# Four head pairs of attention between changes of the matmul tiling, in place of two, in a hand-ordered transformer block

## The chip, the cores and the metric

The kernel runs on one core of a Trainium2 chip. The metric is device time in microseconds for one launch; smaller is better. The core has five engines, each with its own queue, which it works off in the order written: TensorE (PE in the profile, with its weight loads as PEld), VectorE (DVE), ScalarE (ACT), GpSimd (POOL), and SyncE (SP), which only issues DMAs. An instruction waits for semaphores of other engines, and everything behind it in its queue waits with it.

## The reference

Input x has 8 batches of 512 rows of 256 floats. Four residual blocks follow each other, each behind a layer norm:

```python
x = x + attn_a(ln(x))   # Q,K,V = x W; Q,K l2-normalised; Q * mean over rows of (K*V)
x = x + ffn(ln(x))      # r = sigmoid(xr W_r); k = relu(xk W_k)^2; r * (k W_v)
x = x + attn_b(ln(x))   # 16 heads of 64; softmax over the *queries* (axis=2)
x = x + ffn(ln(x))      # the same weights as the first ffn
```

In the ffn, xr and xk mix each row with the row before it. In `attn_b`, scores are q.k/8, the softmax runs over the query axis for each key, and the 16 head outputs are joined and projected from 1024 to 256 columns. All is float32. `attn_b` has 8 x 16 heads of 512 x 512 scores and is the largest part.

## The kernel before

**Attention.** Heads are worked in pairs, 8 pairs to a batch, 64 pairs in all. A pair is four steps of 128 keys. In one step `scores` (L1262) issues 64x64-tiled matmuls that put two heads' scores, keys by queries, into one PSUM tile of two banks; VectorE finds the maximum of each row for both heads with one reduction of 1024 (L1279); `exps` (L1284) has ScalarE write two exponentials of 512 and their sums (L1290). Since the softmax runs over the queries, the sums belong to keys: `scale_v` (L1298) divides the values by them, a reciprocal on VectorE (L1303) and a product on GpSimd (L1307). `context` (L1314) multiplies scaled values and exponentials in two more banks, and after the fourth step ScalarE copies one (L1334) and VectorE adds the other (L1335). Three score tiles of two banks and the two context banks fill PSUM; full-size matmuls borrow free tiles, one bank of each.

**Everything else** is full-size (128x128) matmuls: `linear` and `queries` (the first attention, L678, L728), `mean` (L748), `ffn` (L559), its second use called the tail (`tail`, L1218), with first products for both halves in `keys` (L600), `project_pairs` (L949: queries and keys of two pairs), `values_fast` (L989) and `project_out_fast` (L1118). The last four use a seven-product scheme of Strassen's kind (`seven`, L893): seven products of half size replace eight, differences of inputs are made beforehand on GpSimd, and the results are put together by ScalarE and VectorE while a bank is used twice. A batch's row differences (`sums_of_rows`, L856, L872) lie in `xts`, of which there is one buffer; those of the context (`differences`, L1090, L1102, and `last_differences`, L1105, L1111) overwrite buffers that the tail uses. Rows are turned into columns through DMA transposes that SP issues (L450, L1205), with copies on GpSimd before and after (L445, L454, L1200, L1209).

**The order.** TensorE must change its tiling between attention and the rest. The main loop (L1397) takes two pairs at a time: `attend` (L1340) issues eight steps of scores, and the contexts four or five steps behind; then full-size work is issued, then the next two pairs. Which full-size work comes, and how all engines' instructions interleave, is decided when the program is built, by the class `Order` (L104): each piece of work is a chain of steps with an engine, an assumed cost and the time at which it may start; `PLAN` gives each kind of chain a due stretch and a lead; `CHOICES` gives each stretch a budget shift and picks that depart from the rule. Nothing is decided on the chip.

```python
for first in range(0, G, 2):
    attend(first)
    ...
    order.add(project_pairs(g + 1), "pairs", g)
    ...
    order.until(g, share)
```

`p` is a pair's number in its batch. Before, two pairs are projected in every stretch; the out-projection of batch b-1 and the second half of the values of b come behind p = 1, the first half of the next batch's values behind p = 3, with due times two and four stretches later.

## Time and profile before

| | us |
|---|---|
| median of 3 runs (lowest, highest) | 1130.21 (1129.76, 1130.29) |
| the profiled execution's own time | 1131.28 |
| its span | 1129.5 |
| TensorE busy | 1108.6 |
| VectorE busy | 784.5 |
| ScalarE busy | 675.3 |
| GpSimd busy | 588.6 |
| DVE reductions L1279, 256 of 1216 ns | 307.7 |
| GpSimd scaled values L1307, 128 of 613 ns | 78.3 |

The page gives busy times by engine, the span in 40 slices, the chain of work that ended last, and groups of instructions by line with what ended the idle time before them. Each float32 matmul stands as two records. The 64x64 records overlap four at a time, and the ends of matmuls are modelled, so lengths are best read from start to start.

### The profile page before, as it was taken

How to read it: one execution, taken by the hardware profiler on the slowest of the kernel's cores; microseconds unless marked ns; L12 is line 12 of the kernel's file. 1: busy time of each engine (PE TensorE's matmuls, PEld its weight loads, DVE VectorE, ACT ScalarE, POOL GpSimd, SP SyncE). 2: the span in 40 equal slices, each digit the busy share in tenths (PEclk: the TensorE clock that was granted, in tenths of full speed). 3: DMA queues.
4: the chain of work that ended last, by engine and by line, in shares of the span. 5: the costliest groups of instructions: out<-in, count | busy, mean ns of one | idle time of the engine just before them, and what ended most of it. 6: DMA issues, size and time to landing. Idle time of an engine off the chain costs nothing. (4 is left out here: it accounts for less than half of the span.)

```text
span 1129.5 us, 19476 instructions
## 1 busy us (share of the span) xinstructions
PE 1108.6 (98%) x6938; PEld 691.4 (61%) x6938; DVE 784.5 (69%) x1487; ACT 675.3 (60%) x1779; POOL 588.6 (52%) x909
## 2 busy tenths in 40 slices
PE   7999999999999999999999999999999999999997
PEld 4655556664756657666567656575565765655556
DVE  5767777668576785777856777657776677765764
ACT  4657656377455773567645776547774377554653
POOL 3594445554465464665557546476553764344311
PEclk9999999999999999999999999999999999999999
DMA  6020100110101111112011110111110111001101
GB/s 228 13 82 11 28 1 10 29 29 11 29 30 38 20 20 29 39 29 29 10 38 38 24 23 17 51 20 38 20 19 20 27 31 20 1 20 28 20 1 38
DMA packets 83424, 34.16 MB, mean 30 GB/s; under 512 B 73088, under 2 KB 81920, under 8 KB 82816
## 3 DMA queue, kind: packets, MB, share of 16 engines
q1 hardware_dynamic: 82432, 31.87, 12.5%
q8 instruction: 55, 0.90, 0.3%
q10 hardware_dynamic: 864, 1.05, 0.3%
q14 instruction: 41, 0.34, 0.1%
q0 software_dynamic: 32, 0.00, 0.0%
HBM read 10.89 MB, written 4.19 MB: 13 GB/s over the span
## 5 line engine op out<-in xcount | busy, mean ns | idle before, releaser
L1290 ACT ACTIVATE e<-sc,nm 128x512 f32<-128x512 f32 x512 | 346.5, 690 | 140.1 <-DVE nm L1279 139.9
L1279 DVE TENSOR_REDUCE nm<-sc 128x2 f32<-128x1024 f32 x256 | 307.7, 1216 | 48.5 <-PE sc L1274 47.6
L1274 PE MATMUL sc<-qk 64*64 64x512 f32 x2048 | 265.1, 593 | 4.6 <-DVE prev_g L486 1.3
L1327 PE MATMUL cx<-e,vs 64*64 64x512 f32 x2048 | 263.6, 590 | 0.8 <-POOL vs L1307 0.5
L1307 POOL TENSOR_TENSOR vs<-v,rs 128x256 f32<-128x256 f32 x128 | 78.3, 613 | 266.2 <-DVE rs L1303 256.5
L1327 PEld LDWEIGHTS cx<-e,vs 64*64 64x64 f32 x2048 | 85.0, 133 | 136.5 <-issue 113.4
L1274 PEld LDWEIGHTS sc<-qk 64*64 64x64 f32 x2048 | 75.3, 132 | 139.6 <-issue 79.6
L1290 ACT ACTIVATION_READ_ACCUMULATOR e<-sc,nm 128x1 f32 x512 | 105.9, 207 | 0.0
L972 ACT ACTIVATE qk<-m_qk,bias 128x256 f32<-128x256 f32 x124 | 51.9, 473 | 45.2 <-PE m_qk L964 45.1
L1335 DVE TENSOR_TENSOR ctx<-cx,ctx 128x512 f32<-128x512 f32 x64 | 44.2, 691 | 47.9 <-ACT ctx L1334 39.5
L980 DVE SCALAR_TENSOR_TENSOR qk<-m_qk,dbias,qk 128x256 f32<-128x256 f32 x124 | 54.1, 478 | 16.7 <-PE m_qk L964 14.3
L699 PE MATMUL kv<-wkv,xrFalse 128*128 128x512 f32 x112 | 53.8, 612 | 0.0
L445 POOL COPY xrFalse<-xnFalse 128x512 uint16<-128x512 uint16 x72 | 41.7, 611 | 8.8 <-ACT xnFalse L418 8.8
L1334 ACT COPY ctx<-cx 128x512 f32<-128x512 f32 x64 | 37.5, 586 | 11.1 <-PE cx L1327 11.1
L454 POOL COPY xrFalse<-xkFalse 128x1024 uint16<-128x1024 uint16 x24 | 31.7, 1337 | 22.8 <-DMA xkFalse<-xrFalse 22.8
L1145 PE MATMUL m_y<-ctx,al 128*128 128x256 f32 x168 | 39.8, 380 | 0.0
L964 PE MATMUL m_qk<-xta,aq 128*128 128x256 f32 x124 | 39.3, 398 | 0.1
L964 PE MATMUL m_qk<-xta,sums_q 128*128 128x256 f32 x124 | 37.7, 386 | 0.3 <-DVE qk L926 0.3
L964 PE MATMUL m_qk<-xts,aq 128*128 128x256 f32 x124 | 37.4, 383 | 0.3 <-DVE qk L916 0.3
L964 PE MATMUL m_qk<-xts,ak 128*128 128x256 f32 x124 | 36.9, 379 | 0.0
L964 PE MATMUL m_qk<-xta,ak 128*128 128x256 f32 x124 | 36.9, 379 | 0.0
L964 PE MATMUL m_qk<-xta,sums_k 128*128 128x256 f32 x124 | 36.9, 379 | 0.0
(272 smaller groups left out, 2119.6 us busy)
## 6 DMA issues: line engine op xcount, KB each, us to landing
out<-x SPq DMA_DIRECT2D x16, 256.0 KB, 2.1
x<-in_x SPq DMA_DIRECT2D x6, 512.0 KB, 4.1
aq<-in_aq SPq DMA_DIRECT2D x1, 1024.0 KB, 7.2
ak<-in_ak SPq DMA_DIRECT2D x1, 1024.0 KB, 9.3
av<-in_av SPq DMA_DIRECT2D x1, 1024.0 KB, 11.4
al<-in_al SPq DMA_DIRECT2D x1, 1024.0 KB, 5.3
xkFalse<-xrFalse SPq DMA_TRANSPOSE x36, 3.1
x<-in_x ACTq DMA_DIRECT2D x4, 128.0 KB, 4.2
```

The source lines that it names most:

```text
L445: nc.gpsimd.tensor_copy(apart.rearrange("p (l k u d) -> p l k u d", l=2, k=KC, u=2)[:, :, :, u, :], xn[:, u, :].rearrange("p (k d l) -> p ...
L699: nc.tensor.matmul(ps, lhsT=xt[:, kc, u * P : (u + 1) * P], rhs=wkv[:, kc, :], start=(kc == 0), stop=(kc == KC - 1),)
L964: nc.tensor.matmul(ps[:, w * HS : (w + 1) * HS], lhsT=lhs[w][n - 1], rhs=block_of_rows(b, n), start=start and w == 0, stop=True, skip_grou ...
L972: nc.scalar.activation(dst[:, w, :], ps[:, w, :], AF.Identity, bias=bias[:, w, p : p + 1])
L980: nc.vector.scalar_tensor_tensor(dst[:, w, :], ps[:, w, :], dbias[:, w, p // 2 : p // 2 + 1], part[:, w, :], ALU.add, ALU.add,)
L1145: nc.tensor.matmul(ps, lhsT=lhs[n - 1][:, g, :], rhs=rhs[g][n - 1], start=first and g == 0, stop=True, skip_group_check=True,)
L1274: nc.tensor.matmul(ps[m * HD : (m + 1) * HD, j, :], lhsT=kt[hs, keys], rhs=qt[hs, :], start=True, stop=True,)
L1279: nc.vector.tensor_reduce(nm, ps, AX.X, ALU.max, negate=True)
L1290: nc.scalar.activation(e[:, j, :], ps[:, j, :], AF.Exp, bias=nm[:, j : j + 1], accum_out=sums[g, h][:, c % 2, j : j + 1],)
L1307: nc.gpsimd.tensor_tensor(vs, vh[b, p // 4][:, 2 * h : 2 * h + 2, cols].rearrange("p t (j d) -> p t j d", j=2), rs.unsqueeze(3).to_broadca ...
L1327: nc.tensor.matmul(cx[m][j * HD : (j + 1) * HD, :], lhsT=vsc[g, c // 2][ks, c % 2, j, :], rhs=es[g, c][ks, j, :], start=(c == 0), stop=(c ...
L1335: nc.vector.tensor_tensor(ct, cx[1], ct, ALU.add)
```

## The change

- The main loop takes four pairs between two stretches of full-size work, except the first two and the last two pairs. `attend(first, n)` holds any number of pairs; a pair's contexts run one step behind the next pair's scores.
- Both `project_pairs` of four pairs come in one stretch, so there are four query/key buffers (`heads`). With stretches behind pairs 1 and 5 alone, the first half of the next batch's values comes behind p = 5, and both halves are due at once.
- PSUM is eight tiles of one bank. A score step takes two of them, and its maximum is two reductions of 512 in place of one of 1024.
- To make room, squares are written over a tile that a later product fills, in place of a scratch tile; one set of `sums` is left out; the value bias is loaded in quarters into `vb` and `dvb`, which a subtraction later turns into a difference; the output bias is loaded late, into the room of `sums_y`, and added by a chain of its own (`biased`).
- `CHOICES` is a new table of 18 rows, one to a stretch. With it the order of nearly all instructions is new.

```diff
@@ -28,6 +28,7 @@
 FFN = 1.1 + 6 * BANK
 FAST = BANK / 2
 CHANGE = 0.1
+STEPS = 18
 PAIRS, BANKS = 3, 2
 X_LANDS = (4.1, 8.5, 12.0)
 PASS = {"T": 0.27, "A": 0.2, "V": 0.17, "G": 0.17, "S": 2.2}
...
@@ -64,9 +62,9 @@
     "ffn 0": (-1, 8), "ffn 1": (-3, 8), "ffn": (-3, 8),
     "norm 0": (-1, 8), "norm 1": (-3, 8), "norm": (-3, 8),
     "rows": (-1, 8), "tail": (15, 0), "keys": (15, 0), "tail last": (17, 16), "tail 6": (17, 0), "keys 6": (17, 0), "pairs": (0, 8),
-    "values 1": (2, 8), "values 0": (4, 8), "y": (0, 8), "y differences": (0, 8),
-    "y rows": (4, 8), "y plain": (2, 0), "y last": (11, 16), "scale": (0, 128),
-    "v 0": (-1, 0), "v 1": (3, 0), "project": (-1, 0), "sums": (0, 0), "late sums": (5, 0), "sums v": (1, 0),
+    "values 1": (0, 8), "values 0": (0, 8), "y": (0, 8), "y differences": (0, 8),
+    "y rows": (4, 8), "y plain": (2, 0), "y last": (11, 16), "scale": (0, 128), "bias": (5, 0),
+    "v 0": (-1, 0), "v 1": (1, 0), "project": (-1, 0), "sums": (0, 0), "late sums": (5, 0), "sums v": (1, 0),
 }
 
 class Steps:
...
@@ -154,9 +152,13 @@
 
     def take_pair(self):
 
-        self.clear(range(PAIRS))
-        since, i = min((t, i) for i, t in enumerate(self.banks[:PAIRS]))
+        self.clear(range(2 * PAIRS))
+        since, i = min((max(self.banks[2 * i : 2 * i + 2]), i) for i in range(PAIRS))
         return i, since
+
+    def keep_pair(self, i, until):
+
+        self.banks[2 * i : 2 * i + 2] = [until, until]
 
     def give(self, i=None):
 
...
@@ -293,7 +295,7 @@
     small = ctx.enter_context(tc.tile_pool(name="small", bufs=7))
     epool = ctx.enter_context(tc.tile_pool(name="epool", bufs=5))
     cpool = ctx.enter_context(tc.tile_pool(name="cpool", bufs=9))
-    heads = ctx.enter_context(tc.tile_pool(name="heads", bufs=2))
+    heads = ctx.enter_context(tc.tile_pool(name="heads", bufs=4))
     psum = ctx.enter_context(tc.tile_pool(name="psum", bufs=1, space=bass.MemoryType.PSUM))
     halves_v = ctx.enter_context(tc.tile_pool(name="halves_v", bufs=4))
     ctx.enter_context(tc.manual_schedule())
...
@@ -338,28 +340,26 @@
     aq = weight("aq", [P, KC, H * HD], nc.sync)
     ak = weight("ak", [P, KC, H * HD], nc.sync)
     av = weight("av", [P, KC, H * HD], nc.sync)
-    vb = const.tile([P, H * HD], F32, tag="vb", name="vb")
-    lb = const.tile([P, 1, D], F32, tag="lb", name="lb")
+    vb = const.tile([P, 2, 2 * P], F32, tag="vb", name="vb")
 
     lc = const.tile([P, KC], F32, tag="lc", name="lc")
     dlc = const.tile([P, 1], F32, tag="dlc", name="dlc")
     dbias = const.tile([P, 2, NP // 2], F32, tag="dbias", name="dbias")
     dvb = const.tile([P, 2, 2 * P], F32, tag="dvb", name="dvb")
-    nc.sync.dma_start(out=vb, in_=a["vb"].partition_broadcast(P))
+    for half in range(2):
+        for dst, at in ((vb, 0), (dvb, 1)):
+            cols = slice((2 * half + at) * 2 * P, (2 * half + at + 1) * 2 * P)
+            nc.sync.dma_start(out=dst[:, half, :], in_=a["vb"][cols].partition_broadcast(P))
     nc.sync.dma_start(out=bias[:, 0, :], in_=a["qb"])
     nc.sync.dma_start(out=bias[:, 1, :], in_=a["kb"])
-    nc.sync.dma_start(out=lb[:, 0, :], in_=a["lb"].partition_broadcast(P))
     nc.sync.dma_start(out=lc, in_=a["lb"].rearrange("(k p) -> p k", p=P))
 
 
     def psum_tile(i, name):
...
@@ -703,8 +704,9 @@
             ready = yield "A", 0.8, ready
             vs = two.tile([P, D], F32, tag="av", name=f"av_{b}_{h}_{u}")
             nc.scalar.copy(vs, ps[:, D:])
-            sq = one.tile([P, D], F32, tag="sq", name=f"sqk_{b}_{h}_{u}")
-            nc.scalar.activation(sq, ps[:, :D], AF.Square, accum_out=ss[:, u : u + 1])
+            nc.scalar.activation(
+                kv[:, u, :], ps[:, :D], AF.Square, accum_out=ss[:, u : u + 1]
+            )
             if u == 1:
                 order.add(queries(b, h), *due_of("queries", b))
...
@@ -811,9 +813,13 @@
                 add_front(b + 1)
 
         if b == B - 1:
-            yield "G", 1.3, ready
-            xh = xb[:, 2 * h : 2 * h + 2, :]
-            nc.gpsimd.tensor_tensor(xh, xh, lb.to_broadcast([P, 2, D]), ALU.add)
+            order.add(biased(b, h, ready), "bias", NP * b)
+
+    def biased(b, h, ready):
+
+        yield "G", 1.3, ready, -1, "lb"
+        xh, lb = x[b][:, 2 * h : 2 * h + 2, :], blocks["sums_y"][:, 0:1, :D]
+        nc.gpsimd.tensor_tensor(xh, xh, lb.to_broadcast([P, 2, D]), ALU.add)
 
 
...
@@ -1188,6 +1199,10 @@
                 out=al.rearrange("p (g i) d -> p g i d", i=2)[:, :, 0, P:],
                 in_=a["al"].rearrange("p (g i) d -> p g i d", i=2)[:, :, 0, P:],
             )
+            nc.sync.dma_start(
+                out=blocks["sums_y"][:, 0, :D], in_=a["lb"].partition_broadcast(P)
+            )
+            order.marks["lb"] = p4 + 2.5
         order.add(rows_of_output(b, 0, max(c11, c21)), "y rows", NP * b + 9)
 
     def rows_of_output(b, h, ready):
...
@@ -1266,20 +1281,21 @@
         if c % 2 == 0:
             sums[g, h] = small.tile([P, 2, 2], F32, tag="sums", name=f"sums_{g}_{h}")
         i, since = order.take_pair()
-        ps = psum_tile(i, f"sc_{g}_{c}")
+        ps = [psum_tile(2 * i + j, f"sc_{g}_{c}_{j}") for j in range(2)]
         for m in range(2):
             keys = slice(c * P + m * HD, c * P + (m + 1) * HD)
             for j in range(2):
                 hs = slice(j * HD, (j + 1) * HD)
                 nc.tensor.matmul(
-                    ps[m * HD : (m + 1) * HD, j, :], lhsT=kt[hs, keys], rhs=qt[hs, :],
+                    ps[j][m * HD : (m + 1) * HD, :], lhsT=kt[hs, keys], rhs=qt[hs, :],
                     start=True, stop=True,
                 )
         nm = small.tile([P, 2], F32, tag="nm", name=f"nm_{g}_{c}")
-        nc.vector.tensor_reduce(nm, ps, AX.X, ALU.max, negate=True)
+        for j in range(2):
+            nc.vector.tensor_reduce(nm[:, j : j + 1], ps[j], AX.X, ALU.max, negate=True)
         ready = order.place("T", 0.86, max(since, order.marks[f"qk_{g - g % 2}"]))
-        scored[g, c] = i, ps, nm, order.place("V", 1.14, ready)
-        order.banks[i] = 1e9
+        scored[g, c] = i, ps, nm, order.place("V", 1.2, ready)
+        order.keep_pair(i, 1e9)
 
     def exps(g, c):
 
...
@@ -1335,30 +1351,26 @@
             nc.vector.tensor_tensor(ct, cx[1], ct, ALU.add)
             ctxt[divmod(g, NP)] = ct
             ready = order.place("A", 0.5, ready)
-            order.banks[PAIRS:] = [ready, order.place("V", 0.62, ready)]
-
-    def attend(g):
-
-        for c in range(NT):
-            if c == 3:
-                order.at_once(scale_v(g, 0))
-            scores(g, c)
-            if g > 0:
-                context(g - 1, c)
-            else:
-                order.fill(BANK)
-            exps(g, c)
-            order.fill(0.0, 1.0)
-        for c in range(NT):
-            scores(g + 1, c)
-            if c == 1:
-                order.at_once(scale_v(g, 1))
-            if c > 0:
-                context(g, c - 1)
-            if c == 3:
-                context(g, 3)
-            exps(g + 1, c)
-            order.fill(0.0, 1.0)
+            order.banks[2 * PAIRS :] = [ready, order.place("V", 0.62, ready)]
+
+    def attend(first, n):
+
+        for g in range(first, first + n):
+            behind = 1 if g > first else 0
+            for c in range(NT):
+                if c == 3 and g < first + n - 1:
+                    order.at_once(scale_v(g, 0))
+                scores(g, c)
+                if c == 1 and g > first:
+                    order.at_once(scale_v(g - 1, 1))
+                if g > 0 and c >= behind:
+                    context(g - 1, c - behind)
+                elif g == 0:
+                    order.fill(BANK)
+                if behind and c == 3:
+                    context(g - 1, 3)
+                exps(g, c)
+                order.fill(0.0, 1.0)
 
 
     G = B * NP
...
@@ -1394,10 +1404,13 @@
     total -= 17 * 1.1 + 7 * 1.1
     total += 2 * FAST - 7 * FAST / 2
     total -= 7 * 2 * FAST
-    for first in range(0, G, 2):
-        g = order.period = first + 1
+    first = 0
+    while first < G:
+        n = 2 if first in (0, G - 2) else 4
+        g = order.period = first + n - 1
+        order.step += 1
         order.place("T", CHANGE, 0.0)
-        attend(first)
+        attend(first, n)
         order.place("T", CHANGE, 0.0)
         order.open = g
         for h in range(2):
@@ -1407,19 +1420,21 @@
             order.add(project_out(b, 0), "y plain", g)
         if p == 1 and b > 0:
             order.add(project_out_fast(b - 1), "y", g)
-        if g + 1 < G:
-            order.add(project_pairs(g + 1), "pairs", g)
+        for i in (1, 3):
+            if g + i < G:
+                order.add(project_pairs(g + i), "pairs", g)
         if p == 1 and b > 0:
             order.add(values_fast(b, 1), "values 1", g)
-        elif p == 3 and b < B - 1:
+        elif p == 5 and b < B - 1:
             order.add(values_fast(b + 1, 0), "values 0", g)
-        share = (total - order.spent) / ((G - first) // 2) + order.choice[0]
+        share = (total - order.spent) * n / (G - first) + order.choice[0]
         begin = order.spent
         order.until(g, share)
         if g < G - 1:
             order.fill(share - (order.spent - begin), 1.0 + order.choice[1])
 
             order.fill(order.marks[f"qk_{g + 1}"] - order.now)
+        first += n
 
     order.fill(order.free["G"] - order.now, 4.0)
```

## The prediction

> **What bounds the kernel now.** I read the page's busy times and slices first, then the chain that ended last, then stretches of the span cut at each change of tiling, then the timelines of VectorE and GpSimd.
>
> ```profile
> span 1129.5 us, 19476 instructions
> ...
> PE 1108.6 (98%) x6938; PEld 691.4 (61%) x6938; DVE 784.5 (69%) x1487; ACT 675.3 (60%) x1779; POOL 588.6 (52%) x909
> ...
> PE   7999999999999999999999999999999999999997
> ```
>
> TensorE is busy from end to end. Nothing can be won but its own gaps and what it pays to change its tiling. The chain of work shows that payment:
>
> ```profile
> 901.38 1.02 PE sc L1274 x8
> ...
> 1001.77 1.72 PE cx L1327 x16
> 1003.48 1.06 PE m_v L1001 x4
> 1004.54 1.73 PE m_y L1145 x8
> 1006.27 0.86 PE m_v L1001 x4
> ```
>
> A piece of four 256-wide matmul records takes 0.86 and eight 64x64 records also take 0.86 (1.72 for sixteen); the first piece after a change takes 1.02 or 1.06. So entering the small tiles costs 0.16 and leaving them 0.20. Stretches tell where more is lost:
>
> ```profile
> 258.45:267.86 9.41, 8.54 (x40) 6.52 (x37) 7.76 (x22) 7.56 (x18) 5.87 (x12) 1.00 0.14 27
> 406.28:420.17 13.89, 13.89 (x129) 4.77 (x128) 10.77 (x13) 11.86 (x32) 8.85 (x16) 1.00 0.11 21
> 556.21:587.45 31.24, 31.24 (x132) 24.24 (x128) 18.80 (x43) 14.82 (x42) 15.10 (x26) 1.00 0.09 18
> 601.35:625.72 24.37, 24.37 (x117) 21.19 (x113) 14.71 (x37) 9.39 (x22) 20.98 (x34) 1.00 0.13 26
> 670.92:679.30 8.38, 8.38 (x40) 6.53 (x36) 6.74 (x19) 7.21 (x17) 5.79 (x11) 1.00 0.17 33
> ```
>
> The columns are the length, then each engine's busy time. The second row is attention (128 records, 13.74 + 0.16: nothing lost). The fourth is full-size work, 112 records at 0.2158 = 24.17, and 0.20: nothing lost. The first holds 36 records, 7.77 + 0.20, and loses 1.44; the last holds the same and loses 0.41. Done for all stretches from the first score on, the 35 full-size ones lose 12.0 beyond their 0.20 (or 0.16) and the 36 attention ones 2.3 beyond their 0.16: 14.3 of waiting in the old order. The full clock (1.00) is granted throughout.
>
> **The change, part by part.** The profiled execution has a span of 1129.5 and took 1131.28, 1.07 above the median of the three runs, 1130.21. I work out differences and put them on that median. Matmuls are the same in number and shape in both orders (6938 records here).
>
> *Fewer changes of tiling.* The old order has 36 round trips between the tilings, the new one 19. 17 x (0.16 + 0.20) = **-6.1**. Both prices are this trace's, and hardly vary.
>
> *The old waits go.* The order is written anew, so all **-14.3** go with it; what the new order waits for must be put in their place. I laid its stretches out at 0.2158 a record and looked for each piece whose input, by the rows below, comes later than TensorE does.
>
> *(a) Out-projection, products 5 and 3.* In six of seven batches they now stand back to back (before, another 0.86 piece stood between them), and 3 adds into the bank that 5's reader on VectorE, L1158, 0.42, must have left. The nearest row is a score behind its last projection:
>
> ```profile
> 266.39 0.59 PE L964 MATMUL m_qk<-xta,sums_k 128*128 128x256 f32 x2
> 267.03 0.69 DVE L936 TENSOR_TENSOR qk<-m_qk,qk 128x512 f32<-128x512 f32 x1 [0.44 <-PE m_qk L964]
> ...
> 267.86 1.09 PE L1274 MATMUL sc<-qk 64*64 64x512 f32 x8 [0.87 <-DVE prev_g L489]
> ```
>
> The last record issues at 266.61 and its slot ends at 266.83; the score comes at 267.86: 1.03, of which 0.16 is the change. With 0.42 for 0.69, 0.87 - 0.27 = 0.6. 6 x 0.6 = 3.6 (ends: 0, if product 4 slipped between; 5.2 at 0.87).
>
> *(b) Out-projection behind the tail.* The tail of batch b-2 and the out-projection of b-1 now share a stretch (behind pair 1). The differences of the context on GpSimd overwrite buffers of that tail, so twelve of them stand between its last product, o_g, and product 6:
>
> ```profile
> 187.01 2.78 POOL L1102 TENSOR_TENSOR xrTrue<-ctx,ctx 128x256 f32<-128x256 f32 x4
> ...
> 194.19 2.78 POOL L1102 TENSOR_TENSOR xkTrue<-ctx,ctx 128x256 f32<-128x256 f32 x4
> ```
>
> Four take 2.78, 0.685 apart. Chain: 0.25 to VectorE, 0.69 (L596), 1.27 (L645), 12 x 0.685 = 8.2, hops 0.1: 10.5. Cover: in three batches five pieces of 1.73 and three of the four groups of product 6 (1.3): 9.9, wait 0.6. In the last such stretch 9.1, wait 1.4; in two 13.4, none. 1.8 + 1.4 = 3.2 (ends: 0, as now, where the tail is a stretch earlier; 10.5 with no cover).
>
> *(c) Two batches' rows in one stretch (behind pair 5).* `xts` has one buffer. Pairs 6 and 7 of a batch and 8 and 9, the next batch's first, are now projected in one stretch, so GpSimd's four L872 (0.73 each) must fall between product 4 of the one and product 6 of the other: three pieces, 2.6, against 2.2 for the three needed, hops, and whatever stands in front of them in GpSimd's queue. Then VectorE falls behind: in such a stretch its queue holds, in 3.9 of TensorE's time, one L936 (0.61), six BN_STATS with their aggregates (0.53 each), L1011 and L916 (0.61 each): 5.0, so that a piece waiting for a bank waits 1.1; kv and gf behind transposes and evictions come later still. Per stretch the latest piece is 1.2, 2.1, 1.6, 0.2 and 1.0 late; 6.1 in all (ends: 0, if lateness is caught up before it counts; 10.5, five at the worst).
>
> *(d) First scores behind evictions.* One stretch ends on projections (0.8, as in the rows above); two others end on kv and q, whose readers on ScalarE and VectorE (L707, L711, L741) hold the banks of the first scores by 1.9 and 0.4. 3.1 (ends: 0, 6).
>
> *(e) Seven products alone.* Five stretches open with a pair's seven products and nothing between them; the stretch of 8.38 above has the same and loses 0.41. 5 x 0.41 = 2.1.
>
> *(f) Attention.* A step of a pair takes TensorE 1.72 and ScalarE 1.33 + 0.12. The reduction becomes two of 512:
>
> ```profile
> 414.08 0.69 DVE L1335 TENSOR_TENSOR ctx<-cx,ctx 128x512 f32<-128x512 f32 x1 [0.27 <-ACT ctx L1334]
> 414.69 2.34 DVE L1279 TENSOR_REDUCE nm<-sc 128x2 f32<-128x1024 f32 x2
> ```
>
> One of 1024 follows another after 1.12; 512-wide work follows after 0.61, so two cost 0.10 more, 26 us of VectorE over 256 steps. Its step goes from 1.37 to 1.47, under 1.72: nothing, while other work stays under 0.25 a step. [...]
> Four stretches start with GpSimd behind, and a context waits for its scaled values (L1307): 0.3 to 0.5 each, 1.5 (ends 0, 4).
>
> *(g) The first attention.* Its full-size pieces between scores go: six score steps in a row now follow ScalarE's 1.33 and not 0.86, 5 x 0.47 = 2.3 (its own old wait is in the 14.3).
>
> *(h) Small ones.* Undisturbed-looking stretches here lose 0.26 in eight cases: 8 x 0.26 = 2.1.
>
> *Costed at nothing:* eight one-bank tiles (no full-size piece here waits for a bank inside a stretch), four query/key buffers (the old pair's scores are past), squares written over the later product (L711 already waits for that ScalarE operation, 23.6 us in all), the value bias as four quarter loads (three more issues on SP of 0.45 each; it landed at 22.3 and is first read at 49.5). The output bias, loaded late on SP behind the reload of `al`, is read by GpSimd in the next attention; in the first place it took 10.2 to land, and were it late, GpSimd's copies for the output rows would stand behind it, up to 10.
>
> New waits: 3.6 + 3.2 + 6.1 + 3.1 + 2.1 + 1.5 + 2.3 + 2.1 = 24.0. Sum: -6.1 - 14.3 + 24.0 = **+3.6**, so 1130.21 + 3.6 = **1133.8**.
>
> **The rivals.** *Faster: the lateness is caught up.* For (c), (d), (f) a late piece makes TensorE late, and what depends on TensorE's own products shifts along; what hangs on GpSimd and VectorE does not. If half of these 10.7 go, and (g) and (h) with their 4.4, 24.0 - 5.3 - 4.4 = 14.3: a gain of 6.1, 1124. It decides from new waits under 20.4. For it: GpSimd is busy only 52%. *GpSimd's queue binds.* If every stretch behind pair 1 paid (b) without cover, 6 x (10.5 - 5) = 33 less 3.2 counted: 1164; with a third of it 1143. For it: 20.98 busy of 24.37 in the row above, which holds such differences. Against: it lost nothing there. *No change,* 1130: new waits of 20.4, by chance. *VectorE binds attention:* with 0.3 of other work a step, 1.77 against 1.72 over 240 steps, 12: 1146. Against: 10.77 busy of 13.89.
>
> **How the numbers follow.** A measurement tells 0.2%, 2.3 us, from no change. My forecast (slower, some 1132.5 to 1140) 0.50; GpSimd's queue 0.08; VectorE 0.03; no change 0.17; faster 0.22. Slower 0.61, same 0.17, faster 0.22. The range takes in the lesser half of the faster case and GpSimd's third: 1125 to 1143.
>
> **What would show it.** 19 round trips at 0.16 and 0.20; m_y's fifth piece followed by 0.6 of waiting for L1158; the sixth waiting for L1102; stretches behind pair 5 ending 1 to 2 late; attention stretches of 27.5 + 0.16 with waits on L1307. Wrong if waits in full-size stretches stay under 12, or if attention takes over 28.5 each.

## The result, and the profile after

The changed kernel takes 1142.28 us (median of 6 runs, 1140.34 to 1144.72); the kernel before took 1129.99 beside it (6 runs, 1129.60 to 1131.24). The ratio is 1.0107, 95% interval 1.0096 to 1.0118: slower, by 12.3 us, where +3.6 was forecast. The time lies inside the range, but above the 1132.5 to 1140 of the case that I had called the likeliest. Its runs spread over 4.4 us, in a lower part (1140.3 to 1141.2) and an upper one (1143.4 to 1144.7), where those of before spread over 1.6. The profiled execution is an upper one (1144.53, span 1142.6), and so is that of a repeat; the last experiment comes back to this.

The head of the page after, and four of its groups (line, engine, operation, out<-in, shapes; then busy time and mean ns; then the idle time before them and what ended most of it):

```profile
span 1142.6 us, 19840 instructions
...
PE 1114.8 (98%) x6938; PEld 716.5 (63%) x6938; DVE 796.0 (70%) x1747; ACT 677.3 (59%) x1779; POOL 589.5 (52%) x909
...
L1295 DVE TENSOR_REDUCE nm<-sc 128x1 f32<-128x512 f32 x512 | 322.4, 680 | 27.5 <-PE sc L1289 25.0
...
L1343 PE MATMUL cx<-e,vs 64*64 64x512 f32 x2048 | 267.2, 590 | 2.9 <-POOL vs L1323 2.7
```

TensorE has the same 6938 records and is still the bound. The 256 reductions of 1024 are now 512 of 512 and keep VectorE busy for 322.4 in place of 307.7: 14.7 more, where I had worked out 26. The 2.7 of idle time behind GpSimd's `vs` is small beside a span of 1142.6, but it is a hint at the step that fails below.

Stretches between changes of tiling show the rest (length, then busy time of PE, PEld, DVE, ACT and POOL, each with the records that fall into the stretch, those that only overlap its edges too; then the granted clock, DMA share, GB/s):

```profile
0.00:66.20 66.20, 55.93 (x180) 32.92 (x180) 39.82 (x113) 31.70 (x83) 30.78 (x66) 0.97 0.40 125
107.28:134.91 27.63, 27.63 (x258) 10.15 (x257) 23.11 (x43) 22.51 (x63) 6.95 (x9) 1.00 0.00 1
461.74:512.75 51.01, 50.44 (x231) 42.23 (x227) 28.75 (x70) 21.92 (x47) 33.15 (x53) 1.00 0.12 32
540.47:572.03 31.56, 29.95 (x120) 21.42 (x117) 20.45 (x52) 15.26 (x42) 22.11 (x39) 1.00 0.18 34
652.37:681.08 28.71, 28.09 (x258) 9.82 (x257) 22.89 (x42) 22.62 (x63) 14.00 (x18) 1.00 0.24 38
```

The second row is attention over four pairs, 256 records: 27.47 + 0.16, nothing lost. The last row is the same work and loses 1.08 more. The third is a stretch behind pair 1: its 226 records need 48.77, and 0.20 for the change, so 2.04 is lost. The fourth, behind pair 5, has 116 records, sixteen of them 512 wide and so worth two: 132 x 0.2158 = 28.49, and 2.87 is lost. The first row is the setup, up to the first score at 66.20; in the profile before, that score comes at 62.49.

Done for every stretch, as the prediction did it for before, the difference of the two spans, 13.1, comes apart like this:

| part | forecast | measured |
|---|---|---|
| 17 round trips between tilings fewer | -6.1 | -6.1 |
| old waits go (full-size 12.0 + attention 2.3) | -14.3 | -14.3 |
| (a) products 5 and 3 | 3.6 | 4.1 |
| (b) product 6 behind its differences | 3.2 | 3.9 |
| (c) row sums, banks and rows behind pair 5 | 6.1 | 6.6 |
| (d) first scores behind evictions | 3.1 | 1.0 |
| (e), (h) and all small waits in full-size work | 4.2 | 7.3 |
| (f) attention, forecast behind the scaled values | 1.5 | 6.5 |
| (g) the first attention | 2.3 | 1.4 |
| setup | not considered | 3.7 |
| the end | 0 | -1.0 |
| sum | 3.6 | 13.1 |

Of the 9.5 that the forecast lacks, 5.0 is (f), 3.7 the setup, 3.1 the small waits; (d) and (g) take 3.0 back.

**The out-projection, (a) and (b).** TensorE's timeline, the reader on VectorE and the differences on GpSimd, of the same stretch behind pair 1 (start, length, engine, line; in brackets the idle time and its releaser):

```profile
499.88 2.77 POOL L1114 TENSOR_TENSOR xkTrue<-ctx,ctx 128x256 f32<-128x256 f32 x4
...
500.65 2.75 PE L1156 MATMUL m_y<-xkTrue,sums_y 128*128 128x256 f32 x8
...
506.69 1.89 PE L1156 MATMUL m_y<-ctx,sums_y 128*128 128x256 f32 x8
508.62 0.43 DVE L1169 TENSOR_TENSOR xnTrue<-m_y,xnTrue 128x256 f32<-128x256 f32 x1 [1.78 <-PE m_y L1156]
...
509.10 1.99 PE L1156 MATMUL m_y<-ctx,sums_y 128*128 128x256 f32 x8 [0.52 <-DVE xnTrue L1169]
```

Product 5 starts at 506.69 and its slots end at 508.42; product 3 starts at 509.10, when the reader of 5's bank is done: 0.68, six times over (4.7 with the 0.10 by which the next records follow late). Product 6 starts at 500.65 and, fed by differences that come 0.69 apart, ends only at 503.24: 2.59 for 1.73. That is 0.79 to 0.86, three times, and 1.43 in the last such stretch.

**Attention, (f).** GpSimd's and SyncE's timeline ahead of a scaled value, and the context that waits for it:

```profile
228.87 1.17 POOL L446 COPY xrFalse<-xnFalse 128x512 uint16<-128x512 uint16 x2
...
230.07 1.23 SPq L451 DMA_TRANSPOSE xkFalse<-xrFalse  x1
...
234.80 1.35 POOL L455 COPY xta<-xkFalse 128x1024 uint16<-128x1024 uint16 x1 [2.96 <-DMA xkFalse<-xrFalse]
...
241.17 1.27 POOL L1230 TENSOR_TENSOR x<-xnTrue,x 128x512 f32<-128x512 f32 x1
...
244.07 0.61 POOL L1323 TENSOR_TENSOR vs<-v,rs 128x256 f32<-128x256 f32 x1
...
244.74 1.09 PE L1343 MATMUL cx<-e,vs 64*64 64x512 f32 x8 [0.70 <-POOL vs L1323]
```

GpSimd stands 2.96 for a transposing DMA, and in its queue that copy and fourteen more operations, of a norm and of the output rows, come before the scaled value. TensorE's context comes 1.35 late. Four attention stretches (at 234.71, 652.37, 930.34 and 1048.46) lose 0.88 to 1.44 in this way, 4.5 of the 6.5. Two others, at 165.75 and 710.50, lose 0.55 and 1.12 by something else: VectorE. At 710.50:

```profile
713.34 0.87 DVE L551 SCALAR_TENSOR_TENSOR xkTrue<-xrTrue,mu,prev_g 128x256 f32<-128x256 f32 x2
714.12 3.67 DVE L1295 TENSOR_REDUCE nm<-sc 128x1 f32<-128x512 f32 x6
...
717.96 0.61 POOL L1323 TENSOR_TENSOR vs<-v,rs 128x256 f32<-128x256 f32 x1 [3.41 <-DVE rs L1319]
```

VectorE still works off the stretch before, and its first maximum starts 3.62 after the attention does; GpSimd has nothing to do for 3.41 and waits for VectorE's reciprocal.

**The setup.** ScalarE, VectorE and TensorE on the way to the first feed-forward product:

```profile
30.39 0.74 DVE L713 TENSOR_TENSOR xnTrue<-kv,av 128x256 f32<-128x256 f32 x2
30.88 0.37 ACT L706 COPY av<-kv 128x256 f32<-128x256 f32 x1 [4.34 <-DVE xnTrue L713]
32.92 0.85 ACT L510 ACTIVATE xkFalse<-tr_f,omu 128x255 f32<-128x255 f32 x2
34.53 0.88 DVE L520 SCALAR_TENSOR_TENSOR xkFalse<-tr_f,mu,xkFalse 128x256 f32<-128x256 f32 x2 [2.43 <-ACT xrFalse L510]
35.07 2.02 PE L579 MATMUL k_f<-xkFalse,fk 128*128 128x256 f32 x8 [1.64 <-DVE xkFalse L520]
```

The same product on VectorE (L711 there) came at 26.62 before. In the new order it stands later in VectorE's queue, ScalarE's next copy has to wait 4.34 for the buffer that it writes (`av`, which L713 reads), the mixed rows of the feed-forward stand behind that copy, and TensorE waits 1.64. Then, from 50.2 to 53.6, the setup's matmuls run at a granted clock of 0.50:

```profile
48.00:52.00 4.00, 3.33 (x8) 1.58 (x9) 3.05 (x10) 1.09 (x3) 2.06 (x6) 0.77 0.00 0
51.00:52.00 1.00, 1.00 (x3) 0.48 (x2) 0.22 (x2) 0.51 (x2) 0.78 (x4) 0.50 0.00 0
```

Four 512-wide records start 0.85 apart in place of 0.43 and pay 0.42 each, 1.7. Before, the same records had the full clock, 0.43 apart. Of the setup's 3.7, then, 1.7 is the clock, and 2.0 the order.

### The profile page after: what moved, and what is told of

The parts are those of the page before. It is cut to its first block, busy times and chain, and to the rows that moved or that the text cites. A ratio compares the mean times of both kernels' runs of the same rounds, so it can differ in the third digit from the quotient of the medians.

```text
span 1142.6 us, 19840 instructions
## 1 busy us (share of the span) xinstructions
PE 1114.8 (98%) x6938; PEld 716.5 (63%) x6938; DVE 796.0 (70%) x1747; ACT 677.3 (59%) x1779; POOL 589.5 (52%) x909
## 4 chain that ended last, share of the span: by engine, by line
PE 83%; POOL 8%; DVE 3%; DMA 3%; issue 1%; ACT 1%; POOLq 0%; DVEq 0%; ACTq 0%
PE cx L1343 18%; PE sc L1289 18%; PE m_qk L969 14%; PE m_v L1006 7%; PE m_y L1156 5%; PE kv L700 3%; PE o_g L467 2%; PE k_f L579 2%; PE r_g L467 2%; PE r_f L467 2%; PE o_f L467 2%; PE m_k_g L619 2%; DMA xkTrue<-xrTrue 2%; PE q L467 2%; PE y L467 1%
## 5 line engine op out<-in xcount | busy, mean ns | idle before, releaser
L1295 DVE TENSOR_REDUCE nm<-sc 128x1 f32<-128x512 f32 x512 | 322.4, 680 | 27.5 <-PE sc L1289 25.0
L1289 PE MATMUL sc<-qk 64*64 64x512 f32 x2048 | 269.7, 592 | 1.1 <-DVE qk L941 0.9
L1343 PE MATMUL cx<-e,vs 64*64 64x512 f32 x2048 | 267.2, 590 | 2.9 <-POOL vs L1323 2.7
L1343 PEld LDWEIGHTS cx<-e,vs 64*64 64x64 f32 x2048 | 94.4, 133 | 130.3 <-issue 92.7
L1289 PEld LDWEIGHTS sc<-qk 64*64 64x64 f32 x2048 | 92.4, 133 | 127.1 <-issue 82.1
L985 DVE SCALAR_TENSOR_TENSOR qk<-m_qk,dbias,qk 128x256 f32<-128x256 f32 x124 | 54.1, 478 | 12.3 <-PE m_qk L969 10.8
L646 POOL TENSOR_TENSOR x<-x,xrTrue 128x512 f32<-128x512 f32 x14 | 17.8, 1269 | 63.8 <-DVE xrTrue L597 55.9
L646 POOL TENSOR_TENSOR x<-x,xkFalse 128x512 f32<-128x512 f32 x24 | 30.3, 1270 | 21.2 <-DVE xkFalse L597 13.7
L419 ACT ACTIVATE xnFalse<-x,shift_n,rstd_n 128x256 f32<-128x256 f32 x28 | 15.3, 592 | 38.9 <-POOL shift_n L416 38.9
```

What stands on the lines that cost most here:

```text
L985: nc.vector.scalar_tensor_tensor(dst[:, w, :], ps[:, w, :], dbias[:, w, p // 2 : p // 2 + 1], part[:, w, :], ALU.add, ALU.add,)
L1289: nc.tensor.matmul(ps[j][m * HD : (m + 1) * HD, :], lhsT=kt[hs, keys], rhs=qt[hs, :], start=True, stop=True,)
L1295: nc.vector.tensor_reduce(nm[:, j : j + 1], ps[j], AX.X, ALU.max, negate=True)
L1343: nc.tensor.matmul(cx[m][j * HD : (j + 1) * HD, :], lhsT=vsc[g, c // 2][ks, c % 2, j, :], rhs=es[g, c][ks, j, :], start=(c == 0), stop=(c ...
```

## The experiments

### What the split reduction costs, alone and with one-bank tiles

The prediction costed two parts at nothing: the split of the maximum, and the eight one-bank tiles. The first kernel is the kernel before with only the split, still on a tile of two banks:

```diff
-        nc.vector.tensor_reduce(nm, ps, AX.X, ALU.max, negate=True)
+        for j in range(2):
+            nc.vector.tensor_reduce(nm[:, j : j + 1], ps[:, j, :], AX.X, ALU.max, negate=True)
```

> The kernel before with its own order, instruction for instruction, but each score reduction of 1024 written as two of 512 on the same two-bank tile. The prediction's step (f): VectorE's step goes from 1.37 to 1.47 and stays under TensorE's 1.72, so nothing: 1128 to 1132. Rival, VectorE or the later bank release binds attention: each of the 36 attention stretches loses 0.15 to 0.35, which is 5 to 12: 1135 to 1142, and the stretches of 13.89 become 14.05 to 14.25.

Measured: 1138.18 (1137.48 to 1139.00), ratio 1.0067 [1.0054, 1.0079]. The split alone costs 7.7. One attention stretch of two pairs, and the step in it that loses:

```profile
92.58:106.75 14.17, 14.17 (x129) 5.10 (x128) 12.72 (x25) 11.30 (x31) 3.85 (x7) 1.00 0.10 20
...
103.20 0.68 ACT L1291 ACTIVATE e<-sc,nm 128x512 f32<-128x512 f32 x1
...
104.02 0.21 PEld L1274 LDWEIGHTS sc<-qk 64*64 64x64 f32 x8 [0.83 <-ACT e L1291]
```

23 of the attention stretches of two pairs take 14.14 or 14.15, where 13.89 was the rule. A score waits until ScalarE's second exponential has left the tile; the maximum that this exponential needs came later. "Under 1.72: nothing" was therefore wrong for these tiles: the step's sum fits, but its chain, from scores over maximum and exponential back to a free tile, does not.

The second kernel keeps the staging and the order of before, step for step, with the split and one-bank tiles. In it the order is written out, as lists of steps, in place of being planned; full-size work takes one bank of each score pair, as it did:

```diff
+    def written(self):
+        for key in next(WRITTEN).split():
+            self.run(next(c for c in self.chains if c.key == key))
...
-        shape = [P, 2, 512] if i < PAIRS else [P, 512]
-        return psum.tile(shape, F32, tag=f"ps{i}", name=name)
+        return psum.tile([P, 512], F32, tag=f"ps{i}", name=name)
...
+        ps = [psum_tile(2 * i + j, f"sc_{g}_{c}_{j}") for j in range(2)]
...
+        for j in range(2):
+            nc.vector.tensor_reduce(nm[:, j : j + 1], ps[j], AX.X, ALU.max, negate=True)
```

> The kernel before with its staging and its order kept step for step, but the two reductions of 512 now stand on two score tiles of one bank each (full-size pieces still use five of the eight banks), so that a score matmul waits for one half's exponential and not for both. Theory 1 (the prediction: reductions and tiles both cost nothing; the 8 lost in the run with split reductions alone came from something else): no change against that run, 1136 to 1140. Theory 2 (the loss there was a score waiting for the second exponential of a two-bank tile, put off by the longer reductions; the one-bank tile takes it away): back to 1126 to 1131, with attention stretches of 13.89 again.

Measured: 1129.29 (11 runs, 1128.48 to 1130.59), ratio 0.9993 [0.9984, 1.0002]. The same stretch:

```profile
92.96:106.85 13.89, 13.89 (x129) 4.94 (x128) 12.64 (x25) 11.41 (x31) 3.85 (x7) 1.00 0.11 21
```

So the two parts cancel: +7.7 for the split, -8.9 for the tiles. The cost of nothing was right for the two together, for a reason that the prediction did not have: it named VectorE's spare time, and what matters is that a bank comes free after its own exponential. That this is the way in which the tiles help is argued from the row above; the runs show the two amounts.

### How much the hand-picked order is worth

Both kernels carry a table of picks. Here it is emptied in the kernel before and in the changed one:

```diff
-CHOICES = (
...
+CHOICES = ((0, 0, 0, ()),)
```

> The kernel before with its list of choices emptied: the planner takes its own first choice everywhere, with no shifted shares, no reshuffled ties and no forks. Theory 1 (the list carries the old time, and the loss of the changed kernel lies in the order written for it): far slower than 1130, by 50 to 110, with full-size stretches that lose 1 to 4 each. Theory 2 (the staging sets the time and the list is a detail): within 15 of 1130.

> The changed kernel with its list of choices emptied in the same way, to stand beside the kernel before without its list. Theory 1 (four pairs between changes of tiling are worth the 6 of the round trips, and what the changed kernel loses is the order picked for it): faster than the kernel before without its list, by 3 to 20, although both are far slower than 1130. Theory 2 (the staging itself costs: two batches' rows in a stretch, less filler): slower than that by 5 to 30.

Measured: 1234.01 (1232.70 to 1238.35), ratio 1.092 [1.0903, 1.0938], for the kernel before without picks, and 1225.00 (1224.05 to 1225.69), ratio 1.0831 [1.0815, 1.0848], for the changed one. The table is worth 104 in the one and 83 in the other. Without picks the new staging is ahead by 9. That is no clean measure of the staging: the tiles differ too, and the planner fails in different places (44 of attention waits in the one, 7 in the other; 63 and 96 in full-size work; 14 and 18 in the setup), at a granted clock of 0.983 and 0.974, which is part of these losses. It does say what the comparison of the two kernels mostly compares: two tables, each found for its own staging.

### The same staging with another order

If the losses are the order's, other orders must take them away. This kernel has the instructions of the changed kernel in another order: it is written out as a list, as in the kernel above, and the list is the changed kernel's with single steps moved, each move judged by laying the queues out with the trace's durations.

> The changed kernel with all of its instructions, tiles, buffers, staging and its 19 round trips, in another written order: single steps are moved within their stretch where TensorE is late (GpSimd's copies behind the value scaling, out-projection products apart, rows' differences ahead of norms, the setup). Theory 1 (the loss is the order, not the staging): the waits beyond the changes of tiling fall from 31 to about 20, 1125 to 1131, faster than the changed kernel by 11 to 17. Theory 2 (four pairs of attention and two batches' rows in a stretch force the waits; moved, they come back elsewhere): 1137 to 1143.

Measured: 1134.03 (7 runs, 1133.48 to 1134.60), ratio 1.0031 [1.0020, 1.0042]: 8.3 of the 12.3 are the order's. That lies between what the two theories named. Attention waits fall from 7.9 to 3.8, full-size waits from 22.9 to 19.0, and the setup's loss by 2.2, of which 1.7 is the half clock that this profile does not have. What did not move is the out-projection, where six waits of 0.68 and 3.9 at product 6 stand as in the changed kernel. This order leaves 3.9 over the kernel before (1130.13 beside it).

Two parts of that list alone, in the changed kernel's own order: first eight steps of the setup, then a few GpSimd steps of the attention stretches, put behind the scaled values. A line of the list names the chain whose next step is issued; of each list a few moves are shown.

```diff
 front_ffn:0,0
+front_ffn:0,0
 front:0,1
-front_ffn:0,0
+linear:1,1
 front_ffn:0,1
-linear:1,1
...
```

> The changed kernel with its written order kept from the first scores on; only in the setup, before the first attention, eight steps stand elsewhere (the feed-forward's ScalarE and VectorE steps of the first rows ahead of a query piece). Theory 1 (the changed kernel's setup is 3.7 longer because TensorE waits 1.8 for the first feed-forward product and then runs at a granted clock of 0.66 for 5 us; both follow from the order of the setup): 2 to 4 come back, 1138 to 1140.5, and no run's mean clock lies below 0.999. Rival (the lower clock comes by chance, and what the setup gains is lost in front of the first scores): 1141 to 1143.5, some runs at 0.998.

```diff
-front_norm:5,0
 project_out_fast:3
...
 front_norm:5,1
-rows_of_output:3,1
-rows_of_output:3,0
+front_norm:5,0
...
-front_norm:7,0
 rows_of_output:5,0
```

> The changed kernel with its written order kept but for eight steps: in the attention behind pairs 6, 33, 49 and 57 a copy of output rows on GpSimd, or a step in front of it, stands behind the value scaling instead of ahead of it. Theory 1 (a context waits for its scaled values because such a copy of 1.3 stands ahead of them in GpSimd's queue; 0.6 + 1.1 + 0.9 + 1.1 at these four): 2.5 to 4 come back, 1138 to 1140. Rival (GpSimd is behind as a whole, and the wait moves to the next context or to the following full-size stretch): 1141 to 1143.5.

Measured: 1141.65 (4 runs, 1141.03 to 1141.81), ratio 1.0094 [1.0079, 1.0109], for the setup, and 1142.33 (4 runs, 1139.65 to 1142.45), ratio 1.0093 [1.0077, 1.0110], for attention. The medians fall by 0.6 and not at all: both lie where the rivals had put them. The profiles show gains all the same. In the setup's the loss falls from 10.6 to 7.8 (1.0 of it because the full clock came sooner at the start, at 10.20 in place of 12.62), with the half clock still there, as the rival had said:

```profile
48.00:52.00 4.00, 3.98 (x10) 1.66 (x9) 2.56 (x10) 2.38 (x5) 2.29 (x7) 0.60 0.00 0
```

In the other, two attention stretches that had lost 1.24 and 1.28 (at 652 and 1048) lose 0.16, which is the change of tiling, while two others lose 0.26 and 0.18 more, and the full-size stretches 0.6 more in all. Both gains are below the 4.4 over which runs of the changed kernel spread, so one median against another could not settle them. The changed kernel itself, once more beside the next runs:

> The changed kernel, nothing edited: its six runs lay in two groups, 1140.3 to 1141.2 at a mean clock of 0.999 or 1.000 and 1143.4 to 1144.7 at 0.998, and the profiled one, of the upper group, shows TensorE at half clock from 50.2 to 53.7. Theory 1 (the half clock in the setup comes in some executions only and is what parts the groups): again two groups 3 apart, and a profile of the lower group has no value matmuls at double length near 50. Rival (the groups differ by something else): a profile of the lower group shows the half clock as well, or none of the upper group does.

Measured: 1143.02 (4 runs, 1140.55 to 1144.87), ratio 1.0108 [1.0094, 1.0121].

### The old staging with an equally searched order

The kernel with one-bank tiles and the old staging, its list searched in the same way:

> The kernel before with its staging (two pairs between changes of tiling) and the one-bank score tiles of the earlier run, in another written order: single steps moved within their stretch, as was done for the changed kernel. It asks whether the reordering favours the new staging or either. Theory 1 (any written order can still be bettered, and the old staging as much as the new one): 2 to 5 below the 1129.3 of the same kernel in the old order, 1124.5 to 1127.5, and so faster than the kernel before. Theory 2 (the old order is about as good as this staging allows, and its remaining waits, 0.85 each in front of first scores, are forced): 1128 to 1130.

Measured: 1128.13 (11 runs, 1127.24 to 1128.97), ratio 0.9977 [0.9968, 0.9986]. It beats both kernels, and lies in the range of Theory 2. So the comparison at equal effort is 1128.1 against 1134.0, and the question is what the new staging loses beside the 6.1 that it wins.

### Product 5 ahead of product 2

In the changed kernel, with its order kept, one exchange in `project_out_fast`:

```diff
+        i5, ps5, p5 = yield from product(5, ("y", b, 1))
+        c22 = yield from add(c[1][1], ps5, c[1][1], max(p5, u3))
         _, _, p2 = yield from product(2, None, ps1)
...
-        i5, ps5, p5 = yield from product(5, ("y", b, 1))
-        c22 = yield from add(c[1][1], ps5, c[1][1], max(p5, u3))
         _, _, p3 = yield from product(3, None, ps5)
```

> The changed kernel with one exchange in the out-projection: product 5 comes before product 2 (1, 6, 7, 5, 2, 3, 4), so that product 2, 1.73 of TensorE, stands between product 5 and product 3, which adds into the bank that the reader of 5 must have left. All else in the order is kept; the last differences, which follow product 2, come one piece later. Theory 1: the six waits of 0.68 between products 5 and 3 are a loss of their own, 4.1 with nothing behind them; they go, and the time falls from 1143 to 1138.5 to 1139.5. Theory 2 (rival): product 5 now needs its differences one piece earlier and product 4 gets its own one piece later; GpSimd gives a group every 2.8 and TensorE takes a piece every 1.73, so in the four stretches where product 6 already waits, product 5 waits 1 to 2 more, and product 4 waits where the last differences come late; the time stays at 1141.5 to 1145, with the waits on another piece.

Measured: 1141.65 (4 runs, 1139.59 to 1143.10), ratio 1.0093 [1.0079, 1.0107]. The stretch that was shown above:

```profile
497.35 2.76 PE L1803 MATMUL m_y<-xkTrue,sums_y 128*128 128x256 f32 x8
...
502.15 1.99 PE L1803 MATMUL m_y<-ctx,sums_y 128*128 128x256 f32 x8 [0.32 <-DVE xnTrue L1816]
503.98 1.89 PE L1803 MATMUL m_y<-ctx,al 128*128 128x256 f32 x8
505.70 1.89 PE L1803 MATMUL m_y<-ctx,sums_y 128*128 128x256 f32 x8
```

Product 3 follows product 2 without a gap, so the six waits are gone; in three stretches product 5 now waits 0.48 for VectorE, which is a bank's reader and not the differences that the rival named. All waits on these products fall from 4.7 to 1.8. Ratio against ratio the gain is 1.6, within the spread of the runs, and less than the 2.9 of its profile: attention waits rise from 7.9 to 9.6 in it. The time, 1141.65, lies in the rival's range and not in Theory 1's, 1138.5 to 1139.5. The rows speak for the mechanism of Theory 1, with a smaller size, and against the rival's: no product waits longer for its differences than before.

The exchange and a search of the whole order together:

> The changed kernel's staging with the exchange of products 5 and 2 and with the written order of all steps searched again from that of the reordered kernel (same instructions, other places in the queues). Question: what keeps the new staging, with a good order, at 1134.0, where the old staging with one-bank tiles and an equally searched order has 1128.1. Theory 1: the out-projection, 8.6 of waits in the reordered kernel, 4.7 between products 5 and 3 and 3.9 before product 6, because differences, products and readers share one stretch; with the exchange and the order both go to under 2, and the time falls to 1127.5 to 1130.5, level with the old staging or below. Theory 2 (rival): with half as many stretches, what VectorE and GpSimd must do in one of them is more than TensorE covers, wherever the out-projection stands; the waits move to the first scores, to the row sums and to the scaled values, and the time stays at 1132 to 1135.

Measured: 1130.04 (11 runs, 1128.52 to 1131.68), ratio 0.9992 [0.9984, 1.0001]. Theory 1 had the range right, though the waits at product 6 did not go (3.7; 1.2 are left at the others). The new staging can be level with the kernel before. It is still behind the old staging with the same tiles and an equal search, 0.9992 against 0.9977. The effort is not quite equal: the new staging has had a second search and the exchange. By the two profiles (spans 1128.4 and 1126.1), the new staging has -6.1 of round trips, +4.6 of full-size waits, +3.1 of attention waits, +1.4 in the setup (its profile has the half clock there, the other has not) and -0.7 at the end: 2.3 behind, as the spans are. So half as many changes of tiling bring the 6.1, and the fuller stretches between them cost about as much and a little more. A better order than the ones found is not ruled out.

### Where the half clock and the spread come from

Seven matmuls are added to the setup of the changed kernel, in the gaps where TensorE waits, into banks that the next real product overwrites:

```diff
+    def keep_busy(ps, n):
+        for i in range(n):
+            nc.tensor.matmul(ps, lhsT=fk[:, 0, :P], rhs=fv[:, 0, :], start=True, stop=True)
...
+        if name == "n0" and h == 0:
+            keep_busy(ps[:, 0, :], 4)
...
+            if b == 0 and half == 0 and t == 0:
+                keep_busy(ps[:, :256], 3)
```

> The changed kernel with seven matmuls of 128x256 added in the setup, into banks that the next real product overwrites, so that no result changes: four (0.86) ahead of the transposes at 47.5, where TensorE waits 0.74, and three (0.65) ahead of the first product of values at 49.2, where it waits 0.68. They cost at most 0.2. Theory 1: the half clock at 50 to 54 comes of TensorE's light load just before (2.3 to 2.6 busy of 4); with the gaps filled it is busy 3.6 of 4, the full clock stays, the setup loses 1.7 less, and the runs fall in one group at 1140 to 1141.3, median 1140.7, in place of two groups (1140.3 to 1141.2 and 1143.4 to 1144.9) with their median at 1142.3 to 1143. Theory 2 (rival): the half clock does not hang on this load; it comes in the profile as before, and the two groups stay, median 1142 to 1143.2.

Measured: 1141.46 (5 runs, 1140.38 to 1141.68), ratio 1.0091 [1.0077, 1.0105]. TensorE's load and clock around the place, in this kernel:

```profile
44.00:48.00 4.00, 4.00 (x21) 3.49 (x20) 3.65 (x9) 1.69 (x3) 1.32 (x4) 1.00 0.00 0
48.00:52.00 4.00, 4.00 (x17) 2.57 (x15) 3.13 (x11) 1.55 (x3) 2.43 (x7) 1.00 0.00 0
```

The same two windows of the changed kernel:

```profile
44.00:48.00 4.00, 3.10 (x15) 2.25 (x13) 3.65 (x10) 2.13 (x4) 1.32 (x4) 1.00 0.00 0
48.00:52.00 4.00, 3.33 (x8) 1.58 (x9) 3.05 (x10) 1.09 (x3) 2.06 (x6) 0.77 0.00 0
```

The clock stays full, and all five runs lie within 1.3, where those of the changed kernel spread over 4.4. With useless work on TensorE none of the five is an upper run. The first theory holds, as far as five runs can show it; the median is 0.8 above what it named, and the kernel before stood 1.0 above its usual time beside these runs (1130.98). The changed kernel's ten runs fit: the five with a mean granted clock of 0.998 took 1143.4 to 1144.9, the five with 0.999 or 1.000 took 1140.3 to 1141.9. In the two kernels of this staging with a searched order the clock does not part the runs (1133.57 and 1130.26 at 0.997, among 1133.5 to 1134.6 and 1128.5 to 1131.7). The profile of the exchanged products, a lower run (1140.48) with the setup of the changed kernel, has no half clock there either and loses 7.85 in the setup in place of 10.6. So the dip follows the same gaps in some executions and not in others.

Ahead of the dip TensorE waited in parts, 2.1 in all between 46.4 and 49.2. In the trace of the changed kernel the full clock is on record from 12.62, 0.50 of it from 50.16, the full clock from 53.58 and 0.50 from 1142.43; in that of the kernel before, the full clock from 12.75 and 0.50 from 1128.90. The later times lie 11, 12 and 331, and 327, times 3.413 behind the first. The dip lasts one such length. The 3.41 ahead of it, and a stretch of the same length with the same waits in the profile of the exchanged products, which has no dip:

```profile
46.75:50.16 3.41, 1.84 (x7) 0.94 (x8) 3.13 (x8) 1.68 (x3) 0.61 (x2) 1.00 0.00 0
...
44.62:48.03 3.41, 1.96 (x10) 1.05 (x8) 3.06 (x7) 1.60 (x3) 0.97 (x3) 1.00 0.00 0
```

TensorE is busy for 1.84 in the one and 1.96 in the other, a small difference, and a stretch of the changed kernel with 1.77 busy (33.10 to 36.51, with the 1.64 of waiting for the first feed-forward product) had no dip behind it. So the load of the 3.41 just before does not decide it alone; what does is not shown.

The clock explains 1.7 of the difference between lower and upper runs, and not all. The setup's first products run slower too: in the changed kernel's profile their 512-wide records start 0.85 apart up to 12.62 and 0.43 behind it. That costs 2.1 in this profile and 1.0 in the profile of the exchanged products. The filled kernel's profile also loses 2.4 less in attention. Its stretch that answers to the one at 234.71 above has the same order and no wait:

```profile
227.46 1.17 POOL L453 COPY xrFalse<-xnFalse 128x512 uint16<-128x512 uint16 x2
...
231.81 1.33 POOL L462 COPY xta<-xkFalse 128x1024 uint16<-128x1024 uint16 x1 [1.38 <-DMA xkFalse<-xrFalse]
...
241.05 0.63 POOL L1332 TENSOR_TENSOR vs<-v,rs 128x256 f32<-128x256 f32 x1
241.94 1.04 PE L1352 MATMUL cx<-e,vs 64*64 64x512 f32 x8
```

From the end of the copies to the landing it is 3.2 here and 4.8 in the changed kernel's profile (230.04 to 234.80). That difference stands in GpSimd's queue, and the scaled value with its context inherits it: this stretch alone loses 1.4 less. The 4.8 was no exception: from issue to landing the same transposition took 4.6 to 4.9 in four profiles (the changed kernel, its repeat and the two part lists) and 3.1 in this one. So part of what this profile gains over the changed kernel's is this landing and not the clock. Why one transposition took 1.6 longer than the other is open.

## Why the prediction was wrong in size, step by step

The sign was right, the mechanism of most terms too, and the sum was 9.5 short by the profiles. The step that failed most is **(f)**, "four stretches start with GpSimd behind ... 0.3 to 0.5 each": four stretches lose 0.88 to 1.44 behind GpSimd, and two more, 0.55 and 1.12, behind VectorE, for which (f) had put nothing. I had looked for GpSimd's arrears at the start of a stretch and priced what a queue of busy time leaves over. What sets the wait in the four is in the middle: a transposing DMA whose landing GpSimd awaits, and the operations between that and the scaled value. The rows that show it were in the trace before, as idle time ahead of the copies, and I had not laid the DMAs out. The rival of GpSimd's queue names 1143 for a third of its case, which is near the time, but by another place: it had the out-projection pay, and that paid 3.9. The stated range reaches up to 1143 because of this rival, so it is luck that the time lies inside it.

**The setup** was not in the sum at all. "The order is written anew" was applied to the 35 stretches from the first score on, and the setup, 62 us with its own order, was taken over as it was. It cost 3.7: 2.0 by the order, nearly all of it at the product shown, and 1.7 by the clock. "The full clock (1.00) is granted throughout" was read off stretches behind the setup.

**(a)** and **(b)** were right: 0.6 a time forecast and 0.68 measured; 0.6 and 1.4 forecast for product 6, and 0.79 to 0.86 and 1.43 measured. The exchange of products showed that (a) can be taken away. **(c)** had the sum right (6.1 and 6.6), with single pieces 0.3 to 1.0 late: 0.59 and 0.95 twice for `xts`, 0.91 for a bank that VectorE had to leave and 0.63 for one of ScalarE's, 0.84 and 0.99 for kv and gf. **(d)** was three times too large: one first score waits 0.84, another 0.11, and no kv or q holds a bank for 1.9. **(e)** and **(h)** were priced as 13 waits of a common size; measured, the rest of the full-size loss is 7.3, most of it in pieces under 0.15. **(g)** was 1.4 for 2.3.

**The old waits and the round trips** went as laid out. But to take away all 14.3 of one order and put in what I could find of the other was the weak form of the sum: waits that are looked for one by one are found in part. The old order leaves 14.3 over; I credited it with all of that and charged the new one for 24.0, and it leaves 30.8 (22.9 in full-size work, 7.9 in attention).

**What was costed at nothing:** one-bank tiles and the split reduction cost nothing only together (-8.9 and +7.7). The output bias is read at 1049.68 with no wait of its own, and no row shows a cost of the four query/key buffers. The squares did not make the setup's wait, which is for VectorE's reader of `av`.

**The rivals.** Of the late pieces that were to be caught up, none were: (c) came out as laid out. VectorE does not bind attention as its rival had it, step by step: nine of the fifteen long stretches take 27.63 to 27.76, and four of the other six wait for GpSimd. The two that wait for VectorE do so for work that it carries over from the stretch before. Five of the fifteen take over 28.5; the prediction had named that, for each of them, as a sign of being wrong. "No change" and "faster" needed new waits of 20.4 or less; there are 30.8 and the setup. With another order the new staging does come to 1130, as the kernel with the exchange and the searched order shows.

## What to carry to other kernels

When an order is searched anew, every stage of it is new, the setup too, and the waits that one finds by hand are a lower bound: price the rest by what the old order leaves over, not by zero. In a strict queue follow the DMAs that its instructions await, since one landing 1.6 later cost a stretch 1.4 here. Look also at what an engine carries into a stretch: VectorE, busy for 70% of the span, began the first maximum of two attention stretches only 3.06 and 3.62 after their first score. A split that fits an engine's spare time can still lengthen the chain that returns a buffer (7.7 in all, here, on two-bank tiles), so look at which buffer the step must give back, and when, before it is called free.

## What the runs showed of the hardware

- In the changed kernel's profile the granted clock was 0.50 from 50.16 to 53.58, behind 2.1 of short waits on TensorE between 46.4 and 49.2, and 512-wide matmul records started 0.85 apart in place of 0.43. In the profile of the exchanged products, with the same setup, it stayed at 1.00 there. With the waits filled (0.86 + 0.65 of added matmuls) it stayed at 1.00 in the profile, and the runs' spread went from 4.4 to 1.3.
- The same transposing DMA, behind the same copies, landed 3.1 after its issue in one execution (the filled setup) and 4.6 to 4.9 after it in four others (the changed kernel, its repeat and the two part lists).
- Two reductions of 512 in place of one of 1024 cost 23 of the attention stretches of two pairs 0.25 or 0.26 each on two-bank tiles (14.14 or 14.15 for 13.89) and nothing on one-bank tiles (13.89), with VectorE as busy in the one as in the other (12.72 and 12.64 of a stretch).
